# q and k of a transformer block as one 3x2-by-3x3 scheme with fifteen products per group, and a program end without GpSimd's DMAs

## The chip, the cores and the metric

The kernel runs on one core of one Trainium2 chip. The metric is the device time of one execution in microseconds (us), as the median of several runs. TensorE is called PE here, VectorE DVE, ScalarE ACT, GpSimd POOL, SyncE SP. Everything is in fp32.

## The reference

The input is x, eight images of 384 channels with 32x32 = 1024 tokens. It passes two blocks:

```python
xn = layernorm(xf, g1, beta1)                       # per token, over 384 channels
q, k, v = split(xn @ w_qkv.T + b_qkv)               # 8 heads of 48
attn = softmax((q @ k.T) * 48 ** -0.5)
x1 = (attn @ v) @ w_proj.T + b_proj + xf
h = gelu(layernorm(x1, g2, beta2) @ w_fc1.T + b_fc1)   # 384 -> 1536
y = x1 + h @ w_fc2.T + b_fc2
...
c = depthwise_conv_7x7(y) + dw_b
t = gelu(layernorm(c, ln_w, ln_b) @ w1 + b1)        # 384 -> 1536
nx = norm(t over tokens) / (mean over channels + eps)
out = y + (gamma * t * nx + beta + t) @ w2 + b2     # 1536 -> 384
```

## The kernel before, in words

**Layout.** Channels lie on the 128 partitions (384 channels are three tiles), tokens along the free dimension, in two halves of 512. A product is one or a few matmuls of 128x128 weights with 128x512 data into one PSUM bank. There are four banks in the pool `ps_o` and two pairs in `ps_s`; a pair serves the attention's scores.

**Fewer products by algebra.** A weight matrix of 3x3 (or 2x3) blocks times data of 3x2 blocks (three channel tiles, two token halves) is computed by fast schemes, in which sums of weight blocks and sums of data blocks are multiplied, and the products are added up by DVE. fc2 (`mlp`, L802) and w2 (`grn_down`, L1224) use a scheme with 15 products for 18 (`by_thirds`, L828); each of their products is four matmuls that PE adds up. The forms of weight blocks that `by_thirds` needs are made once, during image 0, by `prepare` (L1285, `forms` at L1320), and kept in DRAM.

**q and k** (`qk`, L494). Image 0 has a plain form, 36 matmuls. In the other seven images `fast(m)` (L531) does one of the three tiles of q and k together: 11 matmuls through `accumulate` (L355; the matmul is L358), eight sums of 128x512 on DVE (L549) and one copy on ACT (L551 issues the first copy). The sums need four differences of blocks of xn, which `block_differences` (L1032, operation at L1038) makes on DVE while the values are computed; the weights' sums come from `s_qk`, three loads of 256 KB an image. A chain `finishing` (L514) then adds the bias on ACT (`finish`, L505) and starts the small DMAs of `move` (L509), which copy rows that attention needs in another place. Attention (`attention`, L659) computes scores (L670), exp on ACT (L679) and products with v (L690). It calls `last_tile` after two score groups, so the third tile of q and k is multiplied there.

**What sets the order.** The program is unrolled and its order per engine is fixed when it is written: `Flow` (L112) keeps a planned clock that `flow.pe(U)` advances by 0.857 us with each product; side work stands in chains, generators that yield how long to wait. A chain's next step is issued when its due time has come on that clock; `flow.finish(chain)` issues all that is left. So the chains decide where an operation stands in its engine's queue; an engine then runs its queue in that order and waits on semaphores.

**Order of PE's work** in images 1 to 6: w1's products of the previous image (`grn_up`, L1041), values of the next image (L590), w2's products of the previous image (tiles o_p, through L358), q and k of the next image, attention, proj (L612), fc1 (L351), fc2 (tiles fc_p).

**Side work.** The 7x7 convolution of one image runs on DVE (`convolution`, L978, one tap at L1004), paced by `start_conv` (L1550), whose list gives the spacing up to certain steps: `(35, 4.4)` means that up to step 35 the steps stand 4.4 us apart. Seven of 49 taps per channel tile are done by `help_convolution` (L1009): ACT multiplies into one of four buffers (L1025) and POOL issues a DMA that adds it to the sum in SBUF (L1026). Norms and the finishing of results are other chains.

**Weights** come through a ring of nine tiles, loaded by SP (L279) in the order of use; the next load is issued when a tile has been used.

**The end.** Attention leaves out the maximum in its softmax; `low` and `high` keep the range of the sums. After the last output the kernel compares them (L1708 to L1710), loads the result into a register of each engine (L1712) and, if the range was left, runs `exact_path` (L1677) from a conditional at L1713, a loop over all images in the plain form. In these runs it is not entered.

Of the kernel before, what the change touches and what calls it, by code (L numbers as in the profile page):

```python
# [46 lines left out]
F32 = mybir.dt.float32  # L47
# [4 lines left out]
P = 128  # L52
# [39 lines left out]

ORDER = (0, NP - 1, 1, 2)
# [58 lines left out]
def block_kernel(  # L152
# [4 lines left out]
    wqk: bass.AP,  # L157
    wv: bass.AP,
# [20 lines left out]
    quiet = []  # L179
    s_fc2 = dram.tile([P, len(FORMS), 4 * P], F32, tag="s_fc2", bufs=1, name="s_fc2")  # L180
    s_w2 = dram.tile([P, len(FORMS), 4 * P], F32, tag="s_w2", bufs=1, name="s_w2")
    s_qk = dram.tile([P, CT, 4 * P], F32, tag="s_qk", bufs=1, name="s_qk")
# [29 lines left out]
    attn = const.tile([P, NP, NH], F32, name="attn")  # L212

# [40 lines left out]
    class Weights:  # L254
# [17 lines left out]
        def load(self):  # L272
            if self.todo and self.todo[0][0][0] == self.held:
                self.owed += 1
            elif self.todo:
                key, source = self.todo.pop(0)
                t = ring.tile([P, 6 * P], F32, tag="w", name="_".join(str(k) for k in key))
                if source is not None:
                    nc.sync.dma_start(out=t[:, : source.shape[1]], in_=source)  # L279
                self.tiles[key] = t.rearrange("p (k o) -> p k o", o=P)  # L280
# [35 lines left out]

    def plan_qk(tag):
        return [((f"qk_{tag}", m), s_qk[:, m, :]) for m in range(CT)]
# [29 lines left out]
    def linear_half(lhsT, rhs, nk, h, name):  # L348
        ps = o_tile(name)
        for k in range(nk):  # L350
            nc.tensor.matmul(out=ps, lhsT=lhsT(k), rhs=rhs(k)[:, half(h)], start=(k == 0), stop=(k == nk - 1))  # L351
            flow.pe(U)
        return ps

# [139 lines left out]
    def qk(b, xn, weights=None):  # L494
# [36 lines left out]
        def fast(m):  # L531
            b11, b12, b21, b22, b31, b32 = (xn[:, s, half(n)] for s in range(CT) for n in range(2))
            t1, t2, t3, t4 = (attn[:, i, :] for i in range(4))
            a11, a12, a13, _, a22, a23 = (wqk_sb[:, k, i * CT + m, :] for i in range(2) for k in range(CT))
            sums = weights.at(f"qk_{b}", m)
            s1, s2, s3, s4 = (sums[:, k, :] for k in range(4))
            c11, c12, c21, c22 = (parts[:, i, m, half(n)] for i in range(2) for n in range(2))
            if m < CT - 1:
                p5 = ps_s.tile([P, 2, NH], F32, tag="s", name=f"qk_{b}_{m}_5")[:, 0, :]
            else:  # L540
                p5 = o_tile(f"qk_{b}_{m}_5")

            def product(*pairs):
                bank = o_tile(f"qk_{b}_{m}")
                accumulate(bank, list(pairs))
                return bank

            def plus(dst, bank, part):
                nc.vector.tensor_tensor(dst, bank, part, ALU.add)  # L549

            nc.scalar.copy(c21, product((a11, b11)))  # L551
            plus(c11, product((a13, b31), (a12, b21)), c21)
            accumulate(p5, [(s1, t1)])
            plus(c21, product((s2, t2)), c21)
            plus(c12, p5, c21)
            plus(c12, product((s4, b22), (a13, b32)), c12)
            chains[0, m] = flow.spawn(finishing(0, m))
            plus(c21, product((s3, t3)), c21)
            plus(c22, p5, c21)
            plus(c21, product((a23, b31), (a22, t4)), c21)  # L560
            plus(c22, product((a23, b32)), c22)
            weights.used(f"qk_{b}", m)
            chains[1, m] = flow.spawn(finishing(1, m))

        def last_tile():

            if weights:
                fast(CT - 1)
                return
            for h in range(2):  # L570
                finish(1, CT - 1, linear_half(*args(1, CT - 1), h, f"qk_{b}_last_{h}"), half(h))
            move(1, CT - 1)

        for m in range(CT):
            if weights:
                if m < CT - 1:
                    fast(m)
                continue
            for i in range(2):
                if (m, i) != (CT - 1, 1):  # L580
                    plain(i, m)
# [207 lines left out]
    def difference(dst, more, less):  # L789

        nc.scalar.mul(dst, less, -1.0)
        nc.gpsimd.dma_start(out=dst, in_=more, accum_op=ALU.add)
# [35 lines left out]
    def by_thirds(xt, hid, e, made, weights, wname, column, done, name):  # L828
# [40 lines left out]
        def adding(dst, src):  # L869
            for i in range(2):  # L870
                nc.gpsimd.dma_start(out=dst[i], in_=src[i], accum_op=ALU.add)
# [413 lines left out]
    def prepare(weights, aside):  # L1285
# [17 lines left out]
        def load_blocks(w, name, *which):  # L1303
            t = one.tile([P, CT, N], F32, tag="acc", name=name).rearrange("p c n -> p (c n)")
            parts = []
            for j, (m, k) in enumerate(which):
                parts.append(t[:, j * 4 * P : (j + 1) * 4 * P])
                nc.gpsimd.dma_start(out=parts[j], in_=block_of(w, m, k))
            return parts

        def spare(name):
            return three.tile([P, NH], F32, tag="res", bufs=4, name=name)

# [6 lines left out]
        def forms(name, w, store):  # L1320
            def keep_form(i, t):
                nc.gpsimd.dma_start(out=store[:, i, :], in_=t)

            a11, a12, a31, a33, a13, a23 = load_blocks(w, f"{name}_a", (1, 1), (1, 2), (3, 1), (3, 3), (1, 3), (2, 3))
            x, y, z = (spare(f"{name}_{k}") for k in "xyz")
            yield 16.0
            add(a23, a23, a33)
# [21 lines left out]
            a21, a22, a31, a32, a33, a12 = load_blocks(w, f"{name}_b", (2, 1), (2, 2), (3, 1), (3, 2), (3, 3), (1, 2))  # L1349
            x, y = spare(f"{name}_v"), spare(f"{name}_w")  # L1350
            nc.gpsimd.dma_start(out=x, in_=block_of(w, 2, 3))
            yield 25.0
            add(x, x, a33)
            sub(y, a22, x)
            keep_form(7, y)
            add(a12, a12, a21)
            add(a12, a12, a31)
# [51 lines left out]
        t = one.tile([P, CT, N], F32, tag="acc", name="qk_sums").rearrange("p c n -> p (c n)")  # L1409
        t = t[:, : 4 * C].rearrange("p (j m o) -> p j m o", j=4, o=P)  # L1410
        a11, a12, a21, a22 = (wqk_sb[:, k, i * CT : (i + 1) * CT, :] for i in range(2) for k in range(2))
        add(t[:, 0], a21, a22)
        sub(t[:, 1], t[:, 0], a11)
        sub(t[:, 2], a11, a21)
        sub(t[:, 3], a12, t[:, 1])
        for j in range(4):
            nc.gpsimd.dma_start(out=s_qk[:, :, j * P : (j + 1) * P], in_=t[:, j])
        yield from forms("fc2", wfc2, s_fc2)
        weights.release()
        t = blocks("w1_sums")  # L1420
# [78 lines left out]

    def main():  # L1500
# [76 lines left out]

        def next_values(b):

            if b < B:  # L1580
                flow.finish(state["norm1"])
                differences = flow.spawn(block_differences(state["xn"]))
                values(b, state["xn"])
                flow.finish(differences)
# [23 lines left out]
        for b in range(B):  # L1608
            if b == 0:
                folding = flow.spawn(after(None, folds(weights), 8))  # L1610
                preparing = flow.spawn(after(None, prepare(weights, False), 4))
                aside = flow.spawn(after(folding, prepare(weights, True), 4))
            q_and_k = qk(b, state["xn"], weights if b else None)
# [3 lines left out]
            else:  # L1617
                acc = state["acc"]
                mlp_by_halves(b, xt, xn, weights, ln2, rest, last_convolution)
            kept[b] = keep(b, xt)  # L1620
            if b + 1 < B:
                acc = state["acc"]
            if b == 0:
                xt = load_x(b + 1, "x")
                flow.finish(preparing)
                start_conv(b, 1.6, (9, 1.65), (17, 4.4))
# [5 lines left out]
            if b < B - 1:  # L1632
                y, gx = grn_up(b - 1, acc, weights, b - 1)
                start_conv(b, 1.6 if b == B - 2 else 1.65, (26, 2.1), (27, 9.0), (35, 4.4))
# [35 lines left out]
        blocks = [(r, part) for r in range(CT) for part in LAST]  # L1670
        grn_down_straight(B - 1, y_last, kept[B - 1], weights, B - 1, B - 1, blocks)

    engines = {nc.tensor.engine, nc.vector.engine, nc.scalar.engine, nc.gpsimd.engine, nc.sync.engine}
    with tc.manual_schedule(engines=engines):
        main()

    def exact_path():  # L1677

        load_wqkv(nc.scalar, nc.scalar)
# [23 lines left out]
    fine = small.tile([P, 2], F32, tag="fine", name="fine")  # L1703
    nc.vector.tensor_scalar(fine[:, 0:1], low, SUM_LOW, None, ALU.is_ge)
    nc.vector.tensor_scalar(fine[:, 1:2], high, SUM_HIGH, None, ALU.is_le)
    nc.vector.tensor_tensor(fine[:, 0:1], fine[:, 0:1], fine[:, 1:2], ALU.mult)
    ps = o_tile("n_fine")
    nc.tensor.matmul(out=ps[:, :1], lhsT=ones, rhs=fine[:, 0:1], start=True, stop=True)  # L1708
    again = small.tile([P, 1], mybir.dt.int32, tag="again", name="again")
    nc.vector.tensor_scalar(again, ps[:, :1], P - 0.5, None, ALU.is_lt)  # L1710
    skip = "a comparison gives 0 or 1"
    seen = nc.values_load(again[0:1, 0:1], min_val=0, max_val=1, skip_runtime_bounds_check_because=skip)  # L1712
    with tc.If(seen > 0):  # L1713
        exact_path()
# [39 lines left out]
def _arrays(i):  # L1754
# [13 lines left out]
    def in_pairs(a):  # L1768
# [4 lines left out]

    wqkv = np.asarray(i["L0_conv_w_qkv"])
    return {
        "x": np.asarray(i["x"]).reshape(B, C, N),
        "vecs": _vectors(i),
        "wqk": rows(np.concatenate([wqkv[:C][DENSE].T, wqkv[C : 2 * C][DENSE].T], 1)),
# [25 lines left out]
```

## Time and profile before

| | us |
|---|---|
| median of 3 runs | 3299.46 (3298.49 to 3303.13) |
| the profiled execution | 3299.18 |
| its span in the trace | 3297.2 |
| PE busy | 3274.5 |
| DVE busy | 2392.0 |
| ACT busy | 1604.5 |
| POOL busy | 484.2 |
| one image in the middle, q/k to q/k | 399.6 |
| q/k products of one image | 28.5 |

The span is the time from the first to the last instruction in the trace; 2.0 us lie around it. PE's granted clock was 0.996 of full speed. A middle image repeats with a period of 399.6 us (q/k starts at 1141.84, 1541.43, 1941.02 us). Rows of the profile name a line of the code and a tile; where a helper is shared (L358), the tile's name tells which stage it is: qk, o_p (w2), fc_p (fc2), h (w1). PE's matmuls of fp32 leave two records each in the chain of work.

### The profile page before, as it was taken

How to read it: one execution, taken by the hardware profiler on the slowest of the kernel's cores; microseconds unless marked ns; L12 is line 12 of the kernel's file. 1: busy time of each engine (PE TensorE's matmuls, PEld its weight loads, DVE VectorE, ACT ScalarE, POOL GpSimd, SP SyncE). 2: the span in 40 equal slices, each digit the busy share in tenths (PEclk: the TensorE clock that was granted, in tenths of full speed). 3: DMA queues.
4: the chain of work that ended last, by engine and by line, in shares of the span. 5: the costliest groups of instructions: out<-in, count | busy, mean ns of one | idle time of the engine just before them, and what ended most of it. 6: DMA issues, size and time to landing. Idle time of an engine off the chain costs nothing.

```text
span 3297.2 us, 38818 instructions
## 1 busy us (share of the span) xinstructions
PE 3274.5 (99%) x14330; PEld 1418.3 (43%) x14330; DVE 2392.0 (73%) x3178; ACT 1604.5 (49%) x2194; POOL 484.2 (15%) x569
## 2 busy tenths in 40 slices
PE   9999999999999999999999999999999999999998
PEld 5344444443344433444344443444434444444455
DVE  4445787887857978579786797767876788879840
ACT  3542663447534375353662636526474355623541
POOL 2111210112110121101111022110220112100000
PEclk9999999999999999999999999999999999999999
DMA  5336732657244663537436374273842647333231
GB/s 198 116 107 153 149 61 71 160 115 151 54 105 134 142 124 57 132 105 173 86 58 146 103 182 76 53 168 92 183 73 58 179 92 172 69 79 89 69 96 43
DMA packets 199110, 368.74 MB, mean 112 GB/s; under 512 B 40768, under 2 KB 46784, under 8 KB 198528
## 3 DMA queue, kind: packets, MB, share of 16 engines
q0 software_dynamic: 80896, 158.63, 26.4%
q1 hardware_dynamic: 117728, 206.83, 20.8%
q8 instruction: 116, 1.90, 0.2%
q10 hardware_dynamic: 288, 0.71, 0.1%
q14 instruction: 82, 0.67, 0.1%
HBM read 187.03 MB, written 34.60 MB: 67 GB/s over the span
## 4 chain that ended last, share of the span: by engine, by line
PE 98%; DVE 1%; DMA 1%; ACT 0%; issue 0%; POOL 0%; SPq 0%; DVEq 0%; POOLq 0%; ACTq 0%
PE fc L351 17%; PE s L670 13%; PE o L690 13%; PE h L358 10%; PE fc_p L358 10%; PE o_p L358 9%; PE qk L358 6%; PE v L590 4%; PE o L1130 4%; PE proj L612 4%; PE h_last L1174 2%; PE h L338 2%; PE qk L338 1%; PE ln_sum L394 1%; PE ln_var L394 1%; PE ln_var L380 0%
## 5 line engine op out<-in xcount | busy, mean ns | idle before, releaser
L1004 DVE SCALAR_TENSOR_TENSOR acc<-pad,vec,acc 128x870 f32<-128x870 f32 (+7 forms) x861 | 963.3, 1154 | 9.1 <-DMA acc<-tap 4.5
L679 ACT ACTIVATE p<-s 128x1024 f32<-128x1024 f32 x512 | 524.0, 1024 | 283.6 <-PE s L670 276.6
L670 PE MATMUL s<-qk 48*64 48x512 f32 x4096 | 541.5, 592 | 0.2 <-ACT qk L505 0.2
L690 PE MATMUL o<-p,v 64*64 64x512 f32 x4096 | 537.7, 589 | 0.0
L351 PE MATMUL fc<-xn,fc 128*128 128x512 f32 x1152 | 502.3, 594 | 0.0
L1026 POOL DMA_DIRECT2D acc<-tap x294 | 253.5, 884 | 1208.9 <-ACT tap L1025 751.4
L351 PEld LDWEIGHTS fc<-xn,fc 128*128 128x128 f32 x1152 | 217.5, 190 | 280.6 <-issue 269.3
L358 PE MATMUL fc_p<-hid,fc 128*128 128x512 f32 x728 | 317.7, 593 | 0.0
L370 ACT ACTIVATE hid<-fc,bfc_f 128x512 f32<-128x512 f32 x192 | 131.3, 686 | 344.3 <-PE fc L351 344.2
L690 PEld LDWEIGHTS o<-p,v 64*64 64x64 f32 x4096 | 163.5, 133 | 278.4 <-issue 270.2
L670 PEld LDWEIGHTS s<-qk 48*64 48x64 f32 x4096 | 159.7, 133 | 277.2 <-issue 221.8
L358 PE MATMUL o_p<-y,w 128*128 128x512 f32 x624 | 270.9, 592 | 0.0
L1075 DVE TENSOR_TENSOR y<-h,y 128x512 f32<-128x512 f32 x288 | 196.7, 689 | 90.0 <-PE h L358 75.4
L1025 ACT ACTIVATE tap<-pad,vec 128x512 f32<-128x512 f32 x294 | 213.0, 734 | 18.6 <-DMA acc<-tap 18.4
L358 PEld LDWEIGHTS fc_p<-hid,fc 128*128 128x128 f32 x728 | 137.7, 190 | 176.5 <-issue 172.4
L358 PE MATMUL h<-acc,w_A 128*128 128x512 f32 x432 | 207.2, 595 | 0.0
L358 PEld LDWEIGHTS o_p<-y,w 128*128 128x128 f32 x624 | 118.0, 190 | 148.7 <-issue 132.0
L1004 DVE SCALAR_TENSOR_TENSOR wqkv<-pad,vec,wqkv 128x377 f32<-128x377 f32 (+24 forms) x288 | 177.2, 684 | 0.6
L631 DVE TENSOR_TENSOR attn<-o,attn 128x512 f32<-128x512 f32 x64 | 44.1, 689 | 166.9 <-ACT attn L629 166.9
L796 ACT COPY pad<-x 128x512 f32<-128x512 f32 x48 | 30.2, 635 | 247.6 <-DVE x L862 191.7
L549 DVE TENSOR_TENSOR qk<-qk,qk 128x512 f32<-128x512 f32 x168 | 114.3, 688 | 37.4 <-PE qk L358 26.9
L612 PE MATMUL proj<-attn,wproj_sb 128*128 128x512 f32 x288 | 127.3, 595 | 0.5 <-DVE attn L657 0.5
(334 smaller groups left out, 3754.2 us busy)
## 6 DMA issues: line engine op xcount, KB each, us to landing
acc<-tap POOLq DMA_DIRECT2D x294, 256.0 KB, 3.5
w_A<-in_w SPq DMA_DIRECT2D x72, 384.0 KB
fc<-s_fc SPq DMA_DIRECT2D x91, 256.0 KB
hid<-hid POOLq DMA_DIRECT2D x42, 512.0 KB, 6.9
fc<-in_wfc SPq DMA_DIRECT2D x54, 384.0 KB
w<-s_w SPq DMA_DIRECT2D x78, 256.0 KB
y<-y POOLq DMA_DIRECT2D x36, 512.0 KB, 7.0
kept<-x SPq DMA_DIRECT2D x8, 1536.0 KB
```

What stands on the lines that cost most here:

```text
L351: nc.tensor.matmul(out=ps, lhsT=lhsT(k), rhs=rhs(k)[:, half(h)], start=(k == 0), stop=(k == nk - 1))
L358: nc.tensor.matmul(out=bank, lhsT=lhsT, rhs=rhs, start=k == 0, stop=k == len(pairs) - 1)
L590: nc.tensor.matmul(out=ps[:, :C], lhsT=xn[:, k, t * P : (t + 1) * P], rhs=wv_sb[:, k, :], start=(k == 0), stop=(k == CT - 1),)
L612: nc.tensor.matmul(out=ps, lhsT=wproj_sb[:, m, ct * P : (ct + 1) * P], rhs=attn[:, m, :], start=(m == 0), stop=(m == CT - 1),)
L670: nc.tensor.matmul(out=s[64 * i : 64 * i + 64, j, :], lhsT=kT[64 * j : 64 * j + HD, m, k0 : k0 + 64], rhs=qT[64 * j : 64 * j + HD, m, half ...
L679: nc.scalar.activation(p, s, AF.Exp)
L690: nc.tensor.matmul(out=outs[i][64 * j : 64 * j + 64, :], lhsT=v[keys, t, at : at + 64], rhs=p[keys, j, :], start=(t == 0), stop=(t == KT - 1),
L1004: nc.vector.scalar_tensor_tensor(dst, window, tap, dst, ALU.mult, ALU.add)
L1025: nc.scalar.mul(t.rearrange("p (h w) -> p h w", w=W), window, tap)
L1026: nc.gpsimd.dma_start(out=acc[:, ct, half(h)], in_=t, accum_op=ALU.add)
L1075: nc.vector.tensor_tensor(dst, bank, part, ALU.add)
L1130: nc.tensor.matmul(out=ps, lhsT=tiles[k], rhs=y(k, part), start=(k == 0), stop=(k == HT - 1))
```

## The change

**q and k.** The three tiles of q form one group and those of k another. Each is a 3x3-by-3x2 block product and is done by the scheme of `by_thirds` with 15 products, each a single matmul: 30 an image. `SINGLY` is the order of the products. `BANKS` says which of them share a PSUM bank: the first one of a bank starts it, each later one goes on adding to it, after the intermediate sum has been read. `SUMS` says what is read after each product, and by whom (a text without a sign or with a leading minus is ACT, the rest is DVE): 22 DVE operations and 10 ACT operations an image. The k group is interrupted after product 9 (its thirteenth) for attention's first two score groups; `last_tile` does the remaining two.

**Sums of xn.** `thirds_of` makes ten sums and differences of 128x512 on DVE, in a chain without fixed due times (`yield 3.0`) from the start of values; it must be finished before q and k.

**Weights of q and k.** `prepare` makes 15 forms of both groups from a new input `wqkt`, between fc2's forms and w1's sums, with POOL's loads and stores, in place of four DVE operations and four stores at its start. An image loads six tiles of 128x640.

**Convolution.** The pace list's last entry `(35, 4.4)` becomes `(28, 26.0)`, in image 0 `(17, 4.4)` becomes `(10, 24.0)`.

**The end.** In the exact path, `difference` and `adding` use DVE in place of ACT and of POOL's accumulating DMAs. The comparison is split: `whether_fine` after the last attention block's MLP, `whether_again` before the last products. The branch carries a hint that it is likely taken (that is, that the path is jumped over).

```diff
+SINGLY = (6, 10, 3, 5, 12, 2, 0, 11, 1, 4, 14, 7, 9, 8, 13)
+BANKS = {"n": (6, 5, 0, 4, 9), "z": (12, 11, 14, 8), "k": (10, 7), "q": (2, 1), "j": (3,), "m": (13,)}
+SUMS = {
+    6: ("c11=n",),
+    10: ("c12=k",),
+    3: ("c32=j+c12",),
+    5: ("c12=n+c12",),
+    12: ("c12=z+c12",),
+    2: ("c21=-q",),
+    0: ("c32=n+c32",),
+    11: ("c22=z",),
+    1: ("c31=q",),
+    4: ("c31=n+c31",),
+    14: ("c21=z+c21",),
+    7: ("c22=c22-k",),
+    9: ("c22=c22-n", "c21=c21-n"),
+    8: ("c11=z+c11",),
+    13: ("c12=m+c12",),
+}
...
+        steps = (
+            (e, b11, b12, ALU.subtract),
+            (h, e, b31, ALU.subtract),
+            (e2, h, b12, ALU.add),
+            (h2, h, b32, ALU.add),
+            (f, e, b21, ALU.subtract),
+            (g, b22, f, ALU.add),
+            (g2, g, b32, ALU.add),
+            (f2, f, b12, ALU.add),
+            (f3, f2, g2, ALU.subtract),
+            (d, g2, b31, ALU.subtract),
+        )
...
+        for slot, n in enumerate(SINGLY):
+            bank = next(name for name, members in BANKS.items() if n in members)
+            first = BANKS[bank][0] == n
+            at = banks(bank)
+            nc.tensor.matmul(
+                out=at,
+                lhsT=weights.at(wname, g, slot // 5)[:, slot % 5, :],
+                rhs=rhs[n],
+                start=first,
+                stop=True,
+                skip_group_check=not first,
+            )
+            if slot % 5 == 4:
+                weights.used(wname, g, slot // 5)
...
+            flow.pe(U)
+            behind(n)
+            yield n
...
+            def behind(n):
+                if n in (4, 9, 13):
+                    m = (4, 9, 13).index(n)
+                    chains[i, m] = flow.spawn(finishing(i, m))
...
+        if weights:
+            for _ in fast(0):
+                pass
+            rest_of_k = fast(1)
+            for n in rest_of_k:
+                if n == 9:
+                    break
+            return parts[:, 0], parts[:, 1], last_tile, ready
...
     def difference(dst, more, less):
 
+        if exact[0]:
+            nc.vector.tensor_tensor(dst, more, less, ALU.subtract)
+            return
         nc.scalar.mul(dst, less, -1.0)
         nc.gpsimd.dma_start(out=dst, in_=more, accum_op=ALU.add)
...
-        for j in range(4):
-            nc.gpsimd.dma_start(out=s_qk[:, :, j * P : (j + 1) * P], in_=t[:, j])
         yield from forms("fc2", wfc2, s_fc2)
         weights.release()
+        yield from forms("qk", wqkt, s_qk, 2)
...
-                differences = flow.spawn(block_differences(state["xn"]))
+                state["thirds"] = flow.spawn(qk_thirds(b, state["xn"]))
                 values(b, state["xn"])
-                flow.finish(differences)
...
-                start_conv(b, 1.6 if b == B - 2 else 1.65, (26, 2.1), (27, 9.0), (35, 4.4))
+                start_conv(b, 1.6 if b == B - 2 else 1.65, (26, 2.1), (27, 9.0), (28, 26.0))
...
+    tc.mark_branch_hint_location("exact", "LikelyTaken", engines)
     with tc.manual_schedule(engines=engines):
-        main()
+        again = main()
...
-    with tc.If(seen > 0):
+    with tc.If(seen > 0, label="exact"):
         exact_path()
```

## The prediction

> **What bounds the kernel now.** I read in this order: the page's first part and its fourth (who is busy, who ended last); PE's waits; the chain between 1885 and 1990 us, around the q/k products of one image; the engines' busy time in those stages; the instructions of the program's last lines.
>
> ```profile
> PE 3274.5 (99%) x14330; PEld 1418.3 (43%) x14330; DVE 2392.0 (73%) x3178; ACT 1604.5 (49%) x2194; POOL 484.2 (15%) x569
> PE 98%; DVE 1%; DMA 1%; ACT 0%; issue 0%; POOL 0%; SPq 0%; DVEq 0%; POOLq 0%; ACTq 0%
> ```
>
> PE is the path: a product taken away is time taken away, and every stall of PE that a change adds is time added. PE's waits sum to some 11 us, nearly all of it at the two ends; between images there is none. So two things count: how many products go, and whether the new order makes PE wait where it never did. The chain prices a product:
>
> ```profile
> 1889.65 51.53 PE o_p L358 x120
> 1941.18 18.88 PE qk L358 x44
> 1960.06 1.88 PE s L670 x16
> 1961.94 9.64 PE qk L358 x22
> 1971.58 1.02 PE s L670 x8
> ```
>
> The columns are start, duration, what. A 128x512 matmul leaves two records here, so 66 records are 33 matmuls: (18.88 + 9.64)/33 = 0.864 us each. The stage ahead ("o_p", the second half-MLP of the convolution block, 15 products of four matmuls) and the score groups follow without a gap. Then the other engines, in the o_p stage, the q/k stage, and the start of attention:
>
> ```profile
> core 0: us, PE busy (x) PEld busy (x) DVE busy (x) ACT busy (x) POOL busy (x), PEclk, DMA share, GB/s
> 1886.00:1941.00 55.00, 55.00 (x132) 24.74 (x131) 51.55 (x58) 15.54 (x20) 8.09 (x8) 1.00 0.67 152
> 1941.00:1971.60 30.60, 30.60 (x87) 12.87 (x89) 25.98 (x36) 17.68 (x22) 7.67 (x9) 1.00 0.90 214
> 1971.60:1990.00 18.40, 18.40 (x172) 6.51 (x176) 14.20 (x14) 15.25 (x19) 5.96 (x7) 1.00 0.81 144
> ```
>
> DVE has 3.45 us idle in the 55 us of o_p, although the page says 73% for the whole span. Cut into stretches of 4 us, the idle time lies at 1888 to 1892 (2.4 us) and just before 1897 (0.9 us); from there to 1962 DVE is full. DVE work added in o_p after that is not hidden. It delays DVE operands of o_p's own products, or what comes after them.
>
> The end of the span, the branch after the last output (minimum/median/maximum ns, first and last start):
>
> ```profile
> L1713 PEldq COMPARE_BRANCH  x1: 3809/3809/3809, 3287.4 to 3287.4; - x1
> L1713 POOLq INC_SWDGE_SEM  x1: 1797/1797/1797, 3287.9 to 3287.9; - x1
> L1800 POOLq DRAIN  x3: 51/107/6679, 3289.7 to 3297.0; - x3
> ```
>
> After the branch at 3287.4 the other engines go on only at 3290.7 to 3291.4. POOL increments a semaphore for its DMAs until 3289.7 and then drains for 6.68 us, to 3296.4; the last barrier (0.8 us) ends the span at 3297.2. DVE, the next latest, is through at 3293.7. So POOL sets the end by 2.7 us.
>
> [...] 3.3 to 3.8 us of nothing between the branch and the next instruction. [...] the trace has 688 for L549; independent ones follow each other every 0.60. [...] while an image's 1.57 MB of x came in (1953 to 1961), taps issued by POOL landed up to 9.6 us after issue, against 3.3 at best.
>
> **Part 1, products.** Before: 11 matmuls for each of three tiles, 33 an image. After: 15 for each of two groups, 30. Image 0 uses neither. Removed: 3 x 7 = 21 matmuls x 0.864 = **-18.1 us**, all on the path. This is certain as long as PE stays full.
>
> **Part 2, the sums that feed the products.** Before: four DVE subtractions of xn's blocks (during values). After: ten, in a chain without due dates that starts with values and must be done before q/k. Net six more, 6 x 0.60 to 0.69 = 3.6 to 4.1 us of DVE in values and o_p. The first ones fill the idle 2.4 us, the next the 0.9; what is left over pushes DVE's queue back by 2.0 us by a list of DVE's queue in program order (0.2 after the seventh, then 0.8, 1.4, 2.0 after the last three). Who waits: o_p's sums of blocks. Relative to the stage's start, product 6 starts at 20.63 and its operands are ready at 19.46 and (second pair, needed at 22.35) 21.63; product 12 starts at 41.23, operands at 40.09 and 42.29 (needed 42.95). With PE's own delay taken off, the pairs cost 0.3 + 0.46 and 0.18 + 0.48 = 1.4 us. At q/k's start the last o_p additions on DVE end 0.5 to 0.6 us later than before (about 4.1 after it), the queue's sums of q behind them, and product 5, which goes on in the bank that sum reads, waits 0.27. Together 1.7 us in each of images 2 to 7 (image 1 has no o_p ahead): 6 x 1.7 = **+10.2 us**. Lower end 0 (the scheduler's order puts the extra operations into gaps that I read as full), upper end 6 x 2.7 = 16 (each of the three places costs half as much again).
>
> **Part 3, the q/k stage itself.** DVE does 22 sums for 24; ACT 10 copies for 3, seven more at 0.585 = 4.1 us on an engine that was busy 17.7 of 30.6. Convolution steps (1.15 each) no longer run in this stage: start_conv now stays silent from step 28 for 26 us, instead of going on at 4.4. That empties DVE by about 7 steps = 8 us there, so that the sums that banks wait for are fast; the steps come back 2 to 3 us later than they did, ahead of a deadline tens of us away: nothing. Banks: a product into a bank that goes on must wait for its reader. Spaced by the schedule the reader has 2.6 us or more (three slots) nearly everywhere; ACT starts 0.24 after a product and takes 0.585, DVE 0.2 and 0.69: no wait, except the one priced above. At the end of the k group the last copy and bias (L588 in the changed kernel) are done at 24.0 us after the stage's start, the scores that need them start at 24.3. Slack 0.3; I put 0 to 0.5 an image, **+1 us** in all.
>
> **Part 4, weights.** Six ring tiles of 327 KB for three of 256: with what they displace, 1.18 MB more are loaded inside the q/k stage, where DMA was 90% busy. Products' weights are asked for early enough (nine ring tiles). What can be late is the taps of the helping convolution, see the rivals.
>
> **Part 5, preparation in image 0.** The 15 forms for each group are made once: 13 loads and 15 stores of 128 KB issued by POOL, 18 DVE operations of 256 wide, 28 x 0.85 = 24 us of POOL's queue (15% busy), in place of 4 DVE operations and 4 stores. Behind them stand w1's sums, the folded vectors, then image 0's own accumulating DMAs in fc2. PE at 155 to 161 and 290 to 306 us has the least slack. I take **+4 us**, range 0 to 8; there is no row for it.
>
> **Part 6, the end.** The slow path's DMAs from GpSimd are gone, so POOL has nothing to increment or drain: its 1.8 + 6.7 us go. Next is DVE at 3293.7: the gain is 2.7 us. The compare chain (about 0.5 us of DVE and PE, hidden or not) is computed earlier: another 0 to 1.4. The hint on the branch[...] takes away the 3.3 us too: span end at about 3290.5 to 3291.1. Lower end 0 to -2 (POOL drains anyway), upper -6.7. I take **-6 us**; [...] no row shows it.
>
> **Sum** against the profiled execution (3299.2 = span 3297.2 + 2.0 around it): -18.1 + 10.2 + 1 + 4 - 6 = -8.9, 3290.3. The median of the runs is 0.3 above the profiled one: **3290.5 us**.
>
> **Rivals.** (a) DVE's lag is covered: the extra operations lie in gaps, PE never stalls, preparation hides. -18.1 - 6 = -24, or with small remnants **3276**. For it: the ring of o_p's operands has some 1 us of slack, and one order of DVE more or less decides. Against: DVE 51.55 of 55. Chance 0.20. (b) The hint has no effect (end -2.7) and preparation costs 8: -18.1 + 10.2 + 1 + 8 - 2.7 = -1.6, **3298**: no change. For it: nothing in the trace shows a hint at work. Chance 0.27. (c) Slower: ACT is held by a tap. A tap takes the buffer of the tap four before it, and ACT waits for that one's accumulating DMA to land (before: two waits of 2.5 us in all, landings up to 9.6 us). With 1.18 MB more in the queues at 150 to 400 GB/s, landings move 3 us or more; if the tap stands ahead of ACT's copy for the last k sums, these and the first scores are late by 3.5 us an image, 6 x 3.5 = 21: 3290.5 + 21 = **3311**. It decides once the landing is later than 24.8 us after q/k's start; before, they landed at 21.4 to 23.4. Chance 0.16. (d) The change does what it says only in part: POOL still drains at the end; then the end gives 0 to 2, inside (b).
>
> **How the numbers follow.** The likeliest, 0.37, covers 3284 to 3293. Rival (a) 0.20, (b) 0.27, (c) 0.16. The range leaves (c) out and takes in the whole of the others: low 3275 (-18.1 - 6.7 with nothing back), high 3305 (upper ends of parts 2, 3 and 5 with the small gain at the end). 0.2% is 6.6 us, about what a measurement of this kernel can tell from no change: faster is below 3292.9, with the likeliest and (a) 0.57; same 0.27; slower 0.16.
>
> **What would show it.** Right: PE's matmul records 42 fewer, q/k 25.8 us instead of 28.5; waits of PE on DVE in o_p of 0.2 to 0.5 us, twice a product pair, at products 6 and 12; no INC_SWDGE_SEM and no long DRAIN on POOL; the branch shorter than 1 us. Wrong: q/k products waiting for ACT or DVE in every image (banks), scores waiting for ACT behind a tap (rival c), or gaps of PE of several us in image 0 before 310 us. If PE's waits stay near 11 us, rival (a) holds.

## The result, and the profile after

The changed kernel takes 3347.2 us (median of 4 runs, 3345.2 to 3350.9) against 3299.0 beside it: 1.0144 of the time before, 95% interval 1.0132 to 1.0156. It is 48 us slower; the forecast was 9 us faster, range 3275 to 3305. The profiled execution took 3350.89 us (span 3349.0).

The first part of its page, the columns as before:

```profile
PE 3288.9 (98%) x14288; PEld 1419.3 (42%) x14288; DVE 2417.2 (72%) x3221; ACT 1630.6 (49%) x2243; POOL 498.2 (15%) x593
```

There are 42 matmul records fewer, as the change says, and PE is nevertheless busy for 14 us more. So PE not only waits, it also works more slowly somewhere. PE's waits over the whole execution (total, times, longest):

```profile
PE qk_s L412 <- DVE qk L428: 24.2, 21, 1.9
PE qk_s L412 <- DVE qk L431: 9.6, 7, 1.4
PE ln_sum L477 <- DMA ln_a<-ln_a: 3.6, 2, 2.4
PE ln_var L477 <- DMA ln_sq<-ln_sq: 2.4, 2, 1.6
...
PE o_p L441 <- DVE y L940: 1.3, 6, 0.2
...
PE o_p L441 <- DVE w_e L940: 1.0, 6, 0.2
PE o_p L441 <- PE o_p L441: 1.0, 6, 0.2
```

The kernel before waited some 11 us, at its ends. Here 28 waits, four for each of seven images, stand between q/k products and DVE's sums: 33.8 us. Most of the other new waiting is for DMAs, in front of norms (ln_sum, ln_var). The three lines of o_p are the small stalls that the prediction had. The engines' busy time in o_p, in q/k with its two score groups, and in eight us at q/k's beginning, for the image whose q/k starts at 1574.6:

```profile
core 0: us, PE busy (x) PEld busy (x) DVE busy (x) ACT busy (x) POOL busy (x), PEclk, DMA share, GB/s
1521.60:1574.60 53.00, 52.44 (x121) 22.36 (x120) 51.16 (x59) 12.07 (x14) 7.44 (x7) 1.00 0.65 149
1574.60:1610.50 35.90, 30.99 (x78) 11.68 (x76) 20.24 (x29) 19.27 (x27) 7.49 (x9) 0.95 0.87 216
1577.00:1585.00 8.00, 5.76 (x9) 1.79 (x7) 3.96 (x7) 2.00 (x4) 0.89 (x1) 0.79 0.80 223
```

q/k takes 35.9 us in place of 30.5, with DVE idle for 15.7 of them. The clock column falls to 0.79 in the third row: after the longest wait (1.90 us) the matmuls start 0.85 us apart in place of 0.43, at half speed, for some 3 us. That is a part of the additional busy time.

The difference by stage, from the starts of the stages on PE in the two profiled executions (q/k with its score groups):

| stage | before | after | difference, all images |
|---|---|---|---|
| up to q/k of image 1 | 340.60 | 349.67 | +9.1 |
| q/k of image 1 | 30.49 | 33.81 | +3.3 |
| q/k of images 2 to 7 | 30.49 each | 34.37 to 35.88 | +30.6 |
| o_p beside images 2 to 7 | 51.53 each | 53.04 | +9.1 |
| fc2 and w1 of image 1 | 113.21 | 119.05 | +5.8 |
| last fc1 | 135.79 | 136.98 | +1.2 |
| last w1, h_last and the end | 273.04 | 266.18 | -6.9 |
| the rest | | | -0.4 |
| sum (3349.0 - 3297.2) | | | +51.8 |

The end, as shown of before: first the branch's line, then the line that ends the program.

```profile
L1831 PEldq COMPARE_BRANCH  x1: 415/415/415, 3340.0 to 3340.0; - x1
...
L1831 SPq COMPARE_BRANCH  x1: 70/70/70, 3346.0 to 3346.0; - x1
```

```profile
L1925 POOLq DRAIN  x3: 51/103/3418, 3283.9 to 3348.7; - x3
```

The branch takes 0.4 us for PE where it took 3.8. POOL's increment is gone. Its long drain is not: it takes 3.4 us, but starts at 3283.9, 65 us before the end, as POOL reaches its branch that early. From the last DVE operation to the end of the span it is 3.98 us instead of 10.45.

### The profile page after: what moved, and what is told of

Its sections match the earlier page's. It is cut to its first block, busy times and chain, and to the rows that moved or that the text cites. A ratio compares the mean times of both kernels' runs of the same rounds, so it can differ in the third digit from the quotient of the medians.

```text
span 3349.0 us, 38903 instructions
## 1 busy us (share of the span) xinstructions
PE 3288.9 (98%) x14288; PEld 1419.3 (42%) x14288; DVE 2417.2 (72%) x3221; ACT 1630.6 (49%) x2243; POOL 498.2 (15%) x593
## 5 line engine op out<-in xcount | busy, mean ns | idle before, releaser
L1085 DVE SCALAR_TENSOR_TENSOR acc<-pad,vec,acc 128x870 f32<-128x870 f32 (+8 forms) x861 | 963.5, 1155 | 6.7 <-DMA acc<-tap 1.7
L665 PE MATMUL v<-wqkv,xn 128*128 128x384 f32 x384 | 126.8, 487 | 0.0
```

The costliest lines, as they stand in the source:

```text
L1085: nc.vector.scalar_tensor_tensor(dst, window, tap, dst, ALU.mult, ALU.add)
```

## The experiments

**Where do the waits come from?** These are the instructions around the first wait of an image, out of the trace (start, end, engine, operation, tiles; the numbers in brackets are the products of `SINGLY`, each of which has two records; DVE's last sums of o_p, which end at 1578.67, are left out):

```
1577.200 1577.792 PE  MATMUL        qk_s<-attn,qk    (5, into bank n)
1577.630 1578.222 PE  MATMUL        qk_s<-attn,qk
1578.587 1579.266 DVE TENSOR_TENSOR qk<-qk_j,qk
1579.371 1580.064 DVE TENSOR_TENSOR qk<-qk_s,qk      (reads bank n)
1580.118 1581.131 PE  MATMUL        qk_s<-third,qk   (12, into bank z)
1580.924 1581.985 PE  MATMUL        qk_s<-third,qk
```

Product 12 goes into z, and starts 54 ns after DVE has read n. The weight load ahead of it carries a wait for the semaphore that DVE's sums count up, so the program makes it wait. Both banks carry one name, qk_s: in the q group n and z are the two halves of one pair tile, in the k group j and q. These are the lines of the changed kernel (i is 0 for q, 1 for k):

```python
                    if name in ("nz", "jq")[i]:
                        both_of = ps_s.tile([P, 2, NH], F32, tag="s", name=f"qk_{b}_{i}_s")
                        tiles.update({n: both_of[:, j, :] for j, n in enumerate(("nz", "jq")[i])})
                    else:
                        tiles[name] = o_tile(f"qk_{b}_{i}_{name}")
```

**Theory A**: the program's waits are made per tile, so a product into one half waits for the reader of the other. **Theory B**, nearer to the prediction: DVE comes out of o_p late, still with its last sums, and the readers are late whatever the tiles are.

**1. n and z apart.** The q group takes its banks as the k group does.

```diff
-                    if name in ("nz", "jq")[i]:
+                    if name in ("jq", "jq")[i]:
...
-                        tiles.update({n: both_of[:, j, :] for j, n in enumerate(("nz", "jq")[i])})
+                        tiles.update({n: both_of[:, j, :] for j, n in enumerate(("jq", "jq")[i])})
```

> The changed kernel, in which the q group takes its banks as the k group does: j and q share the pair of PSUM banks, n and z are tiles of their own. Theory A (n and z are halves of one tile, so a product into one half waits for DVE's reading of the other half): the four to five waits of each q group go, with the half-speed matmuls behind the first of them; q/k of one image is 26 to 27.5 us in place of about 35.9 with its two score groups (30.5 before) and the whole is 3347 less 45 to 52, 3295 to 3302. Theory B (DVE is late at the start of the stage, full of o_p's last sums, and the reads are late whatever the tiles are): the first wait of 2 us and the slow matmuls after it stay, three waits of 1 us or less are shortened; 3325 or more.

Measured: 3303.3 us, 1.0013 of before (1.0003 to 1.0023). PE's waits around the same image, o_p and q/k:

```profile
PE qk_s L412 <- DVE qk L428: 0.2, 1, 0.2
PE o_p L441 <- DVE y L940: 0.2, 1, 0.2
PE o_p L441 <- DVE w_e L940: 0.2, 1, 0.2
PE o_p L441 <- PE o_p L441: 0.2, 1, 0.2
```

and its windows of o_p and q/k:

```profile
1497.70:1550.70 53.00, 52.45 (x121) 22.38 (x120) 51.14 (x59) 12.07 (x14) 7.46 (x7) 1.00 0.66 149
1550.70:1579.20 28.50, 28.25 (x81) 11.57 (x79) 20.10 (x29) 19.12 (x26) 5.96 (x7) 1.00 0.95 252
```

q/k is 28.43 us for 35.87, the clock stays at 1.00, and the kernel is 44 us faster than the changed one, a microsecond short of what theory A gave; the 26 to 27.5 us that it gave for q/k were not reached. The wait of 0.2 us that is left is one of the same kind. In this version j and q are the halves of the tile qk_s, and product 2 goes into q:

```
1553.311 1553.903 PE  MATMUL        qk_n<-attn,qk    (5, into bank n)
...
1554.699 1555.380 DVE TENSOR_TENSOR qk<-qk_s,qk      (reads bank j)
1555.436 1556.133 PE  MATMUL        qk_s<-third_e,qk (2, into bank q)
```

Product 2 starts 56 ns after DVE has read j; product 5 doesn't wait.

**2. The k group paired too.** The same two lines with `("nz", "nz")`: a second dose of the suspected cause, where DVE has little to do.

> The changed kernel, in which the k group too has n and z as the two halves of one PSUM pair. In the k group DVE has little to do. Theory A (waits for the reader of the other half): the k group gets about four waits of 0.8 to 1 us and is 15.9 to 17 us long in place of 12.9; with seven images 3347 + 20 to 30. Theory B (late DVE): nothing changes, 3347 within 5 us, since DVE is not late there.

Measured: 3383.4 us in a single run, 36 above the changed kernel's median.

```profile
PE qk_s L412 <- DVE qk L428: 41.2, 42, 1.9
PE qk_s L412 <- DVE qk L431: 9.8, 7, 1.5
PE s L745 <- ACT p L754: 8.0, 7, 1.1
```

Three more waits an image on DVE (42 for 21), 0.8 us each, and one on the scores' pair behind them; q/k is 39 to 41 us. Theory A holds; B would have left the time alone. In the traces q/k grew by 29.5 us over the seven images, the upper end of the expected 20 to 30, with 8 us of waits of the scores among them that the expectation didn't have; fc2 and w1 of image 1 were another 6.6 us longer.

**3. DVE relieved, the pair kept.** The changed kernel with four convolution steps fewer ahead of q/k:

```diff
-                start_conv(b, 1.6 if b == B - 2 else 1.65, (26, 2.1), (27, 9.0), (28, 26.0))
+                start_conv(b, 1.6 if b == B - 2 else 1.65, (22, 2.5), (23, 9.0), (24, 26.0))
```

> The changed kernel as it is (n and z one tile in the q group), with four convolution steps fewer ahead of q and k. DVE's lag is paid for, the shared tile stays. Theory A (shared tile): o_p goes back to 51.5 us; of the four waits in the q group the first falls from 1.9 to some 1.3 us (as in image 1, which has no o_p ahead of it), so that no half-speed matmuls follow; the other three stay at 0.8 to 1.4; q/k 33.8 us, 3347 - 6 x (1.5 + 2.0) = 3326. Theory B (late DVE): the waits fall below 0.5 us together, q/k 29 us or less, 3347 - 50 = 3297.

Measured: 3335.3 us, 1.0110 of before (1.0095 to 1.0126).

```profile
PE qk_s L412 <- DVE qk L428: 19.5, 21, 1.3
PE qk_s L412 <- DVE qk L431: 9.6, 7, 1.4
```

The number of waits is the same. In images 2 to 7 the first one falls from 1.90 to 1.12 us (the 1.3 of the row is image 1's, which was as long before), o_p falls to 51.53 and q/k to 33.6, as theory A had it. The total came out 9 us above the expected 3326: in the profiled execution (3331.9) image 0's fc2 was 4.3 us longer than in the changed kernel's and the last fc1 2.3 us longer, waiting for the convolution that ends later. So late DVE is a part (0.8 us of the first wait), the shared tile is the cause: with DVE relieved q/k is still 39.9 us longer over the seven images than in the next run, which differs from this one only in the tiles.

**4. The same thinning with n and z apart** (the edits of 1 and 3 together). This tests the prediction's part 2.

> The run with n and z apart, with four convolution steps fewer ahead of q and k in images 2 to 7 (22 steps 2.5 us apart, a pause of 9 and one of 26, in place of 26, 2.1, 9 and 26). Theory of the prediction (the six extra DVE operations push DVE's queue back by 2 us in o_p): four steps of 1.15 us pay for them, o_p is 51.5 to 51.8 us in place of 53.04, 6 x 1.3 to 1.5 = 8 to 9 us, 3303 - 8.5 = 3294.5. Rival (the sums of xn delay the operands whatever stands between, as they stand first in the queue): the stall at product 6 stays, half of the gain, 3299.

Measured: 3295.5 us, 0.9986 of before (0.9979 to 0.9992). o_p is 51.53 us in every image, its waits are gone, and q/k 27.92: 2.57 us less than before, that is the three products an image. Four convolution steps (4.6 us) pay for six DVE sums. The rival fell: the stall at product 6 went too. So did the wait of product 2 for j's reader.

**5. Image 1's norms.** fc2 and w1 of image 1 wait for norms. First try: image 0's convolution paced as before.

```diff
-                start_conv(b, 1.6, (9, 1.65), (10, 24.0))
+                start_conv(b, 1.6, (9, 1.65), (17, 4.4))
```

> The run with n and z apart, and image 0's convolution paced as before (17 steps, then 4.4 us apart). That run's image 1 waits for norms' sums that come by DMA (about 5 us, with half-speed matmuls behind them; fc2 and w1 of image 1 are 7.8 us longer than before). Theory P (the silent 24 us put the norm of image 0's convolution and the one behind it at a place of the plan where POOL's queue is full): these waits go, 3303 - 6 to 8, 3295 to 3297. Theory Q (they come from the three products fewer on the plan's clock, or from what the preparation leaves behind): no change, 3303.

Measured on the version with n and z apart: 3306.2 us, 1.0021 of before (1.0011 to 1.0031), so no gain; fc2 of image 1 took 58.3 us against 56.5 and w1 62.3 against 64.1, the same together. Theory P in this form is wrong: the old pace is not what the place of the norm needs.

**6. Both edits together** (the thinning and the old pace of image 0):

> Both edits on the run with n and z apart: if their gains add up, 3303 - 7 - 8.5 = 3287.5, below the kernel before with the new end alone (3293.7). If the earlier steps in image 0 or the later ones in the others make a norm late: 3292 or more.

Measured: 3295.9 us, 0.9983 of before (0.9976 to 0.9990). Nothing is added to the thinning's gain; fc2 of image 1 is 58.7 us.

**7. A shorter pause.** On the thinned version:

```diff
-                start_conv(b, 1.6, (9, 1.65), (10, 24.0))
+                start_conv(b, 1.6, (9, 1.65), (10, 20.0))
```

> The thinned run (n and z apart, four convolution steps fewer ahead of q and k), with image 0's pause 20 us instead of 24. Theory P2 (in image 1 the norm of the convolution comes some 3 to 5 us later on the plan than it did, so that its folding DMAs stand on POOL's queue behind two of fc2's 512 KB additions and land 9.7 us after issue): 4 us earlier puts them ahead again, image 1's fc2 and w1 are 5 to 6 us shorter, 3295.5 - 5.5 = 3290. Rival (the place shifts, but the folds collide with another pair of additions): 3294 to 3297, the waits of norms on DMA in image 1 stay at 4 us or more.

Measured: 3289.5 us, 0.9972 of before (0.9961 to 0.9983). A norm's sum over channels begins with a fold: a DMA of POOL that adds one half of the partitions to the other. The norm's two folds in fc2 of image 1, in the thinned version (4):

```profile
L471 POOL DMA_DIRECT2D ln_sq<-ln_sq x1: 1328/1328/1328, 586.4 to 586.4; - x1
L471 POOL DMA_DIRECT2D attn<-attn x1: 1626/1626/1626, 586.9 to 586.9; - x1
...
DMA to landing us min/median/max: 9.7/9.9/10.2
```

and with the pause of 20 us:

```profile
L471 POOL DMA_DIRECT2D ln_sq<-ln_sq x1: 842/842/842, 583.7 to 583.7; - x1
L471 POOL DMA_DIRECT2D attn<-attn x1: 812/812/812, 585.0 to 585.0; - x1
...
DMA to landing us min/median/max: 3.7/3.9/4.1
```

(3.7 before the change.) In the first case two of fc2's additions of 512 KB were issued on POOL at 584.2 and 585.6, just ahead of the folds; in the second they come at 585.6 and 586.3, behind them. So the folds land 9.9 us after issue behind the additions, and 3.9 ahead of them. fc2 of image 1 is back at 53.93 us, its time before. w1 of image 1 is not: 61.2 against 59.3, with a wait of 0.9 us for another norm's DMA. Together they are 3.8 us shorter than in the thinned version, where 5 to 6 was expected.

**8. The pause of the last convolution beside an attention**, on top of it:

```diff
-                start_conv(b, 1.6 if b == B - 2 else 1.65, (22, 2.5), (23, 9.0), (24, 26.0))
+                start_conv(b, 1.6 if b == B - 2 else 1.65, (22, 2.5), (23, 9.0), (24, 26.0 if b < B - 2 else 20.0))
```

> As the run before it, and in the last convolution beside an attention (image 7's q and k) a pause of 20 us instead of 26. The thinned run's last fc1 is 139.3 us in place of 135.8 before; if that is the convolution that ends later there: 1 to 3 us less, 3288. If the convolution's steps then come back into q and k and make the sums late: q/k of that image over 28.5 us, no gain.

Measured: 3286.9 us, 0.9958 of before (0.9944 to 0.9971). The last fc1 falls from 139.3 to 137.0, q/k stays at 27.92. This is the lowest median measured: 13 us below the kernel before, of which the end alone gives 6.6 (run 9). Its interval overlaps the previous run's, so the medians alone don't show this last step of 2.6 us; the stage does, with 2.3.

**9. The end alone**, on the kernel before: the DVE operations in the exact path, the comparison made earlier, the hint. The diff is cut to the comparison and the hint.

```diff
+    tc.mark_branch_hint_location("exact", "LikelyTaken", engines)
...
+                fine = whether_fine()
...
+        again = whether_again(fine)
...
-    with tc.If(seen > 0):
+    with tc.If(seen > 0, label="exact"):
```

> The kernel before with the change's end alone (no accumulating DMA of POOL in the exact path, the comparison made earlier, the hint on the branch). If the end's gain stands by itself: the time from the last DVE operation to the end falls from 10.5 to 4.0 us, and the whole is 3299.0 - 6.5 = 3292.5. If the gain seen in the changed kernel's end was paid for elsewhere (the hint at the start of the program, where the first values came 0.8 us later): 3293 to 3294.

Measured: 3293.7 us, 0.9981 of before (0.9973 to 0.9989). From the last DVE operation to the end of the span: 4.3 us for 10.5. POOL's long drain takes 6.7 us here as it did before; it starts at 3229.2 now, and nothing waits for it at the end.

**10. The same without the hint:**

> As the run before it, without the hint on the branch. [...] SP stands 3.3 us behind its branch and the whole is 3.3 - 0.5 = 2.8 us slower than with the hint, 3295.3. If the hint does nothing and only POOL's draining was to be saved: the same as with it.

Measured: 3296.2 us, 0.9988 of before (0.9981 to 0.9994). The branch, minimum/median/maximum in ns:

```profile
L1733 PEldq COMPARE_BRANCH  x1: 3369/3369/3369, 3281.3 to 3281.3; - x1
...
L1733 DVEq COMPARE_BRANCH  x1: 72/72/72, 3286.4 to 3286.4; - x1
L1733 SPq COMPARE_BRANCH  x1: 50/50/50, 3287.3 to 3287.3; - x1
L1733 DVEq EVENT_SEMAPHORE  x1: 21/21/21, 3289.7 to 3289.7; - x1
```

Without the hint DVE goes on 3.3 us after its branch, SP (its next line is at 3290.1) 2.8; PE's branch takes 3.4 us. With it these are 0.6, 0.5 to 0.6, and 0.4 to 0.5. The span's tail is 6.0 us for 4.3: the hint is worth 1.7 us in the traces and 2.4 in the medians, whose intervals overlap; the rest of the end's gain, some 4 us, comes from POOL's queue and the earlier comparison, which weren't tried apart. The trace says only this of them: the increment (1.8 us) is gone, and the drain is as long as before, 6.7 us, and stands early because the comparison does.

**11. The preparation alone**, on the kernel before. The diff is cut to the line that runs it; the rest lets `forms` handle these weights and gives them an input and a place in DRAM:

```diff
         weights.release()
+        yield from forms("qk", wqkt, s_qkt, 2)
         t = blocks("w1_sums")
```

> The kernel before, which also makes the 15 forms of q's and k's weights in image 0 and stores them, and doesn't use them (its own q/k sums stay). Prediction: +4, between 0 and 8. If the preparation is what makes image 1's norms late as well: +10 or more, with waits for norms' DMAs in image 1.

Measured: 3300.5 us, 1.0000 of before (0.9991 to 1.0008). fc2 of image 0 is 1.9 us longer (59.0 for 57.2), fc2 and w1 of image 1 are as before (53.93 and 59.28). So the preparation does not make image 1's norms late. How long image 0's attention is differs from one kernel to the next: 124.8 to 127.6 us in three without the preparation, 127.3 to 130.9 in ten with it, one execution each; whether 2 or 3 us of that belong to the preparation is not settled. The median's interval ends at +2.6. But in this run's trace the time from the last DVE operation to the end is 7.4 us for 10.5, though the end is that of before (POOL's drain takes 4.0 us for 6.7). If that holds for all its executions, it hides 3 us of the preparation in the median.

## Why the prediction was wrong

**Part 1, the products, was right**: -18.1 forecast; with no stall left q/k is 27.92 for 30.49, 7 x 2.57 = 18.0.

**Part 2, the sums of xn, was right for o_p**: 1.42 us an image forecast, 1.51 measured, at the four places that were named in products 6 and 12 (0.41, 0.44, 0.18 and 0.49 us for 0.3, 0.46, 0.18 and 0.48; in each the matmul behind the late one is slower too, see the last section). For q/k's start it had the size by luck: 0.27 for product 5, 0.51 measured with n and z apart, but at product 2, which waits for the reader of the other half of its tile. The sum was 10.2, measured 6 x 2.02 = 12.1.

**Part 3 is the step that failed**, at the sentence "Spaced by the schedule the reader has 2.6 us or more (three slots) nearly everywhere". It counted the slots between two products of one bank. The wait belongs to the tile, and in the q group n and z are one tile: products 5 and 12, 0 and 11, 4 and 14, 9 and 8 follow each other directly into its halves. So the second of each two waits at once for DVE to read the one ahead of it: 0.8 to 1.9 us four times an image, where nothing was put for them; the +1 us of this part was for the scores at the k group's end. By the profiled executions q/k is 51.9 us longer than 7 x 27.92. 39.9 of it stays with DVE relieved (run 3); the other 12.0 come from the shared tile and late DVE together, the half-speed matmuls among them. Setting the two apart gave 44 us in the medians. The profile before could not show this, because no stage in it wrote the halves of a pair in turn while another engine read single halves. The code did show it: `both_of`, one allocation, cut in two. The names in the trace (qk_s for both) say the same.

The same part said of the convolution steps that come back later, "ahead of a deadline tens of us away: nothing". That held for images 2 to 6 and failed for image 1: a norm moved behind fc2's large additions on POOL's queue, and fc2 and w1 of image 1 became 5.8 us longer. I looked for the deadline of the convolution and not at what stands beside the norm that follows it. Which of its parts moved it there (the pause, the three products fewer on the plan's clock) is not separated; 4 us less pause put fc2 right, the old pace didn't. What still delays w1 of image 1 by 2 us is open. This is the larger part of what the forecast missed besides the tile: with n and z apart the kernel is 3.0 us above the one before and not 8.9 below, and in the trace fc2 and w1 of image 1 are 7.4 us longer than before.

**Part 4** held where it was sure: no q/k product waits for a DMA in the traces.

**Part 5** (+4, 0 to 8): image 0 was 9.1 us longer in the changed kernel's profile. The preparation alone gave +0.5 in the median, -3 to +2.6; the remainder is mostly attention of image 0. In the ten traces with the preparation, all parts of the change or some, image 0 was 2.7 to 9.1 us longer than before, in the two others 0.3 and 2.4. So the value is neither shown nor refuted.

**Part 6 had the right sum**: -6 forecast, -6.5 in the changed kernel's trace, -6.6 in the median when the end stands alone. Its terms were off in both directions. The hint was put at 3.3 us and was worth 1.7 to 2.4. POOL was to have nothing to drain; it still drained, for 3.4 us in the changed kernel and 6.7 in run 9. By these traces it is off the path because the comparison comes earlier, and not because DMAs are missing. Without the hint DVE stands for 3.3 us behind its branch, with it for 0.6; how the hint does this no view shows.

**The rivals.** (c) named a stall of this kind, a slower kernel through waits in q/k, for another cause: ACT held by a tap. It didn't happen: with n and z apart q/k has no wait for ACT. So (c) had the sign and not the mechanism. (a) fell, as o_p did stall; (b), no change because the hint does nothing, fell with run 10. No rival asked the question "which instructions does each wait cover".

## What to carry to other kernels

Where a schedule lets one engine write one part of a buffer while another reads a second part, look first at what the waits are made for: here a tile of two PSUM banks, not a bank. Two independent sums that are written in turn belong in tiles of their own; the same 30 products with their two score groups then take 28 us and not 36. And here a wait cost more than its own length: the matmul behind it held the next one off for 0.50 to 0.53 us, where they are 0.43 apart otherwise.

## What was unexpected of the hardware

**After a wait of 1.9 us PE ran at half speed for some 3 us, in six of twelve cases.** In the changed kernel six images have a first wait of 1.90 us, and in five of them two to four matmuls behind it start 0.85 us apart in place of 0.43; with the k group paired as well only one of six such waits was followed by any. After the changed kernel's waits of 1.4 us or less the matmuls of q/k were not slowed so: they start 0.53 us apart at most. The row of 1577 to 1585 us above has a clock of 0.79, which is 8 x 0.21/0.5 = 3.4 us at a half. What sets the six cases apart from the other six is not shown.

**A wait at full speed cost about 0.1 us more than itself.** The matmul that follows a wait at full speed here holds the next one off for 0.50 to 0.53 us, where they are 0.43 apart otherwise: in o_p four matmuls start 0.33, 0.33, 0.08 and 0.38 us late, and those behind them make up the rest of the 1.51 us.
